# Softmax sums of an attention kernel: one accumulating chain of transfers instead of three groups of matmuls

## The chip, the cores and the metric

One core of a Trainium2 chip runs the whole program. The metric is device time in microseconds (us). A kernel's time is the median of its runs. One further execution was recorded by the hardware profiler: its trace gives every instruction's start, duration and waits.

## The reference

The input is x of shape 2 x 2048 x 512. The part that matters here is attention with 16 heads of width 32 and 2 groups of keys and values:

```python
q = q * cos + rotate_half(q) * sin          # also k; k and v are shared by 8 heads each
scores = jnp.einsum('bqhd,bkhd->bhqk', q, k_exp) * hd ** (-0.5)
attn = jax.nn.softmax(scores, axis=-1)
out = jnp.einsum('bhqk,bkhd->bqhd', attn, v_exp).reshape(b, s, d)
return out @ wo + bo
```

A layer norm stands ahead of it and a residual addition behind it. A second layer norm and a product with weights that are rounded to 8 bits follow, and another residual addition.

## The kernel before

**Units.** The attention is cut into 64 units: 8 token blocks of 512 queries, 4 quads of heads in each, 2 halves of 256 queries (`HB`) in each quad. A unit runs over all 2048 keys of its batch in 16 chunks of 128 keys, four chunks to a round (`ROUND = 4`, `ROUNDS = 4`). The text calls the rounds of a unit block 0 to block 3. The order of instructions within a round is written out by hand in the program; every engine takes its own instructions strictly in that order.

**A round.** For each chunk PE multiplies the keys with the queries into `T` (L963; in chunks 0 and 1 a matmul with the negated maxima goes ahead, L954), and ACT takes the exponential into a tile `p` of 128 keys x (4 heads x 256 queries) (L972). There are four `p` buffers and two `T` buffers. POOL adds the tiles of two chunks into a tile `pa` (L946, `add_pair`). The first pair's tile is then added to the second pair's by an accumulating transfer that POOL issues (L1015). So a unit leaves four tiles `far_sums[0..3]`, one per round, each the sum of four chunks. In block 2 another accumulating transfer adds `far_sums[0]` to `far_sums[1]` (L1017). The pool of these tiles has four buffers, so a tile of a round is overwritten in the same round of the next unit. At the end of a round PE multiplies the four `p` tiles with the values into `avs[:, 0, :]` (`columns`, L913; 32 records).

**Sums.** The softmax denominators need the sum over the 128 partitions as well. PE does this with a matrix of ones (`sum_up`, L927), 4 matmuls for each tile, into `avs[:, 1, :]` of the next unit: `far_sums[1]` and `far_sums[2]` at the end of that unit's block 0, `far_sums[3]` at the end of its block 1. The trace shows two records for each of these fp32 matmuls.

**Division.** ACT copies the products of a unit into the tile `both[:, 0, :]` at the unit's end (L1033). `finish_heads` copies the sums into `both[:, 1, :]` (L885, ACT), takes reciprocals in two pieces (L889, DVE) and multiplies (L890, POOL) into `attn`. The tile `both` has one buffer:

```python
            both = w2.tile([P, 2, HB], F32, tag="both", name=f"both_{u}", bufs=1)
            nc.scalar.copy(both[:, 0, :], avs[:, 0, :])
            far_before = far_sums
```

**Work ahead and side jobs.** The softmax's maxima for the next unit are found one unit ahead: PE makes scores `s` (L517) and DVE reduces them (L524), 8 pairs of instructions in each round, called at fixed places of the round (`next(scores, None)`). Three PSUM banks hold them, one of which is lent to a side job while that needs it. Side jobs are projections of coming blocks, rope, the output product with `wo`, the second layer norm. They wait in queues, and `fill` takes a step of one where the round has a place for it: `fill(ON_PE)` in the middle of a round, `fill(ON_DVE, 3 if finishing else 2)` at its end. A job of the list `finishing` (the division) goes first. At the start of every second unit ACT splits the next queries into a high part (L246) and POOL subtracts it for the low part (L247). SP's queue carries the other transfers.

Of the kernel before, what the change touches and what calls it, by code (L numbers as in the profile page):

```python
# [13 lines left out]
ALU = mybir.AluOpType  # L14
# [13 lines left out]
def preln_attn_fp8_ffn_kernel(  # L28
# [37 lines left out]
    nc = tc.nc  # L66
# [403 lines left out]
    units = [(k, half) for k in range(len(quads)) for half in range(HALVES)]  # L470
# [28 lines left out]
    def split_maxima():  # L499

        if split:
            mview, mx = split.pop()
            nc.gpsimd.tensor_tensor(
                mview[:, :, :, 1], mx, mview[:, :, :, 0].bitcast(F32), ALU.subtract
            )
# [257 lines left out]
    def fill(kind, pieces=1):  # L763

        for _ in range(pieces):
            ready = [job for job in queue if job.due <= step[0] and not job.waits()]
            if lent[0] is not None:
                ready = [job for job in ready if job is owner[0]]
            able = [
                (jobs, job)  # L770
                for jobs, some in ((finishing, finishing[:1]), (queue, ready), (beside, beside))
                for job in some
                if job.kind in (kind, OTHER) and job.due <= step[0]
            ]
            if able:
                do(*able[0])
# [41 lines left out]
    def stack_next(u):  # L818
        k, half = units[u]
        n, quad = quads[k]  # L820

        if half == 0:
            if k + 1 < len(quads) and k + 1 not in qst:
                while quads[k + 1] not in q_raw:
                    advance()
                stack_queries(k + 1)
        b = batch(k)
        if b + 1 < B and n == (b + 1) * NB - 1 and quad == 2 and half == 1:
            while (b + 2) * NB - 1 not in keys_done:
                advance()  # L830
            fetch_keys("kS", b + 1, 0)
            fetch_keys("dkS", b + 1, 0)
        if b > 0 and n == b * NB and quad == 0 and half == 0:
            fetch_keys("kS", b, 1)
            fetch_keys("dkS", b, 1)
# [69 lines left out]
    def columns(u, chunks, probs, av):  # L905

        k, half = units[u]
        for kc, p in zip(chunks, probs):
            if kc == NTS - 2 and u + 1 < len(units):
                tp = ps_t.tile([P, 4 * HB], F32, tag="E", name=f"mtp_{u + 1}")  # L910
                gather_maxima(u + 1, tp)
            for j in range(4):
                nc.tensor.matmul(  # L913
                    av[j * HD : (j + 1) * HD, :],
                    vX[batch(k)][:, kc, group(k), :],
                    p[:, j, :],
                    start=(kc == 0),
                    stop=(kc == NTS - 1),
                    tile_position=(0, j * HD),
                    skip_group_check=True,  # L920
                )

    def sum_up(dst, parts, start, stop):

        for i, part in enumerate(parts):
            for j in range(4):
                nc.tensor.matmul(  # L927
                    dst[j * HD : (j + 1) * HD, :],
                    ones,
                    part[:, j, :],  # L930
                    start=start and i == 0,
                    stop=stop and i == len(parts) - 1,
                    tile_position=(0, j * HD),
                    skip_group_check=True,
                )

    def add_pair(u, kc, a, b):
        far = kc % ROUND == 2
        pa = papool.tile(
            [P, 4, HB],  # L940
            F32,
            tag="pa" if far else "pair",
            name=f"pa_{u}_{kc}",
            bufs=4 if far else 2,
        )
        nc.gpsimd.tensor_tensor(pa, a, b, ALU.add)  # L946
        return pa

    def probabilities(u, T, kc):

        k, half = units[u]
        if kc < 2:
            for j in range(4):
                nc.tensor.matmul(  # L954
                    T[:, j, :],
                    sel[:, j, :],
                    maxima[u],
                    start=(j % 2 == 0),
                    stop=True,
                    skip_group_check=True,  # L960
                )
        for j in range(0, 4, 2):
            nc.tensor.matmul(  # L963
                T[:, j : j + 2, :],
                stacked["dkS"][:, group(k), kc * P : (kc + 1) * P],
                qst[k][:, j : j + 2, half * HB : (half + 1) * HB],
                start=False,
                stop=True,
                skip_group_check=True,
            )  # L970
        p = ppool.tile([P, 4, HB], F32, tag="p", name=f"p_{u}_{kc}")
        nc.scalar.activation(p, T, AF.Exp, scale=SCALE)  # L972
        return p

    with tc.manual_schedule():
        for _ in range(LEAD):
            next(scores)
        for u, (k, half) in enumerate(units):
            n, quad = quads[k]
            if half == 0 and quad == 0:  # L980
                attn_of[n] = wide.tile(
                    [P, QUADS, TB], F32, tag="attn", name=f"attn_{n}", bufs=2
                )
            stack_next(u)
            banks = [
                ps_t.tile([P, 4, HB], F32, tag="EO"[parity], name=f"T_{u}_{parity}")
                for parity in range(2)
            ]

            far_sums = []  # L990
            whole = u == len(units) - 1
            ending_soon = u >= len(units) - 2
            pieces = 2 if ending_soon else 1
            for r in range(ROUNDS):
                chunks = list(range(r * ROUND, (r + 1) * ROUND))
                step[0] += 1
                while r == 1 and landing:
                    landing.pop()()
                if r == 2:
                    ask(u)  # L1000
                last = r == ROUNDS - 1
                next(scores, None)
                probs = [probabilities(u, banks[kc % 2], kc) for kc in chunks[:2]]
                pair = add_pair(u, chunks[0], *probs)
                next(scores, None)
                if r > 0:
                    fill(ON_PE, pieces)
                probs.append(probabilities(u, banks[0], chunks[2]))
                next(scores, None)
                probs.append(probabilities(u, banks[1], chunks[3]))  # L1010
                if ending_soon:
                    fill(ON_DVE)
                if not (last and whole):
                    far_sums.append(add_pair(u, chunks[2], *probs[2:]))
                    nc.gpsimd.dma_start(out=far_sums[r], in_=pair, accum_op=ALU.add)  # L1015
                if r == 2:
                    nc.gpsimd.dma_start(out=far_sums[1], in_=far_sums[0], accum_op=ALU.add)  # L1017
                fill(ON_PE, pieces)
                next(scores, None)
                split_maxima()  # L1020
                fill(ON_DVE, 3 if finishing else 2)
                if r == 0:
                    avs = ps_av.tile([P, 2, HB], F32, tag="av", name=f"avs_{u}")
                columns(u, chunks, probs, avs[:, 0, :])


                if u > 0 and r == 0:
                    sum_up(avs[:, 1, :], far_before[1:3], False, False)
                elif u > 0 and r == 1:
                    sum_up(avs[:, 1, :], far_before[3:], False, True)  # L1030
                    finishing.append(Job(finish_heads(u - 1, both, avs[:, 1, :])))
            both = w2.tile([P, 2, HB], F32, tag="both", name=f"both_{u}", bufs=1)
            nc.scalar.copy(both[:, 0, :], avs[:, 0, :])  # L1033
            far_before = far_sums
        sums = ps_s.tile([P, TB], F32, tag=s_bank(), name="sums_last")[:, :HB]
        sum_up(sums, [pair, *probs[2:], *far_sums[1:]], True, True)
        finishing.append(Job(finish_heads(u, both, sums)))
        fetch_y_over_keys(2, "kS", 1)
        attending[0] = False
        for jobs in (finishing, queue, beside):  # L1040
            while jobs:
                jobs[0].step()
                if jobs[0].kind is None:
                    jobs.pop(0)
# [122 lines left out]
```

## Time and profile before

| | us |
|---|---|
| median of 3 runs | 2333.15 (2331.62 to 2337.78) |
| the profiled execution | 2336.02 |
| its span, first to last instruction | 2334.2 |

| engine | busy us | share of the span |
|---|---|---|
| PE | 2143.7 | 92% |
| POOL | 1765.1 | 76% |
| DVE | 1698.0 | 73% |
| ACT | 1237.0 | 53% |

The units lie between 127 and 2225 us of the span; most take 33 to 34 us, those without side jobs 28 to 29 us. In that stretch the granted TensorE clock is 0.99. A row of the page's groups has the line, the engine, the operation, the tiles (written <- read), the count, the busy time, the mean of one in ns, and the idle time ahead of them with what ended it. Matmul ends are modelled: a busy PE is not a PE at its peak, and the starts are what can be trusted. Spans on POOL are rough, and neighbouring ones overlap.

### The profile page before, as it was taken

What the parts mean: (1) busy time and instruction counts of PE and PEld (TensorE: products, weight loads), DVE (VectorE), ACT (ScalarE), POOL (GpSimd) and SP (SyncE); (2) the same over time, 40 slices, a digit from 0 to 9 for tenths busy, and PEclk for the clock granted to TensorE, in tenths of its full rate; (3) what the DMA queues carried; (4) which work ended last, traced back from release to release, by engine and by line L of the source; (5) the groups of instructions that cost most, each with busy time, mean ns of one, the idle gap of its engine ahead of it and who ended that gap; (6) DMA issues with size and microseconds to landing.
All of it is one profiled execution on the core that took longest, in us unless ns stands there. A gap on an engine that the chain in (4) does not pass through costs nothing. (4 is left out here: it accounts for less than half of the span.)

```text
span 2334.2 us, 39403 instructions
## 1 busy us (share of the span) xinstructions
PE 2143.7 (92%) x15506; PEld 1242.2 (53%) x15506; DVE 1698.0 (73%) x2679; ACT 1237.0 (53%) x1545; POOL 1765.1 (76%) x1199
## 2 busy tenths in 40 slices
PE   5499999999999999999999999999999899899955
PEld 3255555555555555555555555555555455555522
DVE  3467778776777776876767778676877977767578
ACT  2146556655556555655445456555555555545646
POOL 3268889888878987888868878887888777877810
PEclk9599999999999999999999999999999999999978
DMA  6546656666465765659586456664665645847512
GB/s 204 160 102 128 141 114 161 140 142 131 100 163 130 159 129 136 145 115 197 103 202 137 102 127 136 147 112 96 133 154 123 138 101 115 170 98 197 109 52 112
DMA packets 116411, 312.78 MB, mean 134 GB/s; under 512 B 16896, under 2 KB 17536, under 8 KB 112384
## 3 DMA queue, kind: packets, MB, share of 16 engines
q0 software_dynamic: 50160, 175.66, 40.0%
q1 hardware_dynamic: 63648, 133.21, 19.2%
q8 instruction: 122, 2.00, 0.3%
q10 hardware_dynamic: 2416, 1.38, 0.2%
q14 instruction: 65, 0.53, 0.1%
HBM read 91.56 MB, written 42.99 MB: 58 GB/s over the span
## 5 line engine op out<-in xcount | busy, mean ns | idle before, releaser
L524 DVE TENSOR_REDUCE part<-s 128x1 f32<-128x512 f32 x2048 | 1304.2, 684 | 541.8 <-PE s L517 528.8
L946 POOL TENSOR_TENSOR pa<-p,p 128x1024 f32<-128x1024 f32 x511 | 1234.9, 2466 | 293.1 <-ACT p L972 265.8
L972 ACT ACTIVATE p<-T 128x1024 f32<-128x1024 f32 x1024 | 1001.4, 1024 | 597.8 <-PE T L963 564.6
L517 PE MATMUL s<-kS,qst 128*128 128x512 f32 x2048 | 832.1, 465 | 87.6 <-DVE part L524 28.7
L963 PE MATMUL T<-qst,dkS 128*128 128x512 f32 x2048 | 669.5, 423 | 11.8 <-ACT p L972 11.8
L517 PEld LDWEIGHTS s<-kS,qst 128*128 128x128 f32 x2048 | 369.7, 190 | 478.0 <-DVE part L524 266.5
L913 PE MATMUL avs<-p,vX 128*32 128x256 f32 x8192 | 509.4, 383 | 0.8 <-ACT p L972 0.8
L963 PEld LDWEIGHTS T<-qst,dkS 128*128 128x128 f32 x2048 | 366.0, 189 | 159.8 <-ACT p L972 54.8
L913 PEld LDWEIGHTS avs<-p,vX 128*32 128x32 f32 x8192 | 233.1, 109 | 214.4 <-issue 79.6
L1015 POOL DMA_DIRECT2D pa<-pa x255 | 224.2, 879 | 80.3 <-POOL pa L946 75.6
L301 PE MATMUL po<-wo_sb,attn 128*128 128x512 f32 x256 | 130.7, 596 | 1.3 <-POOL attn L890 1.3
L889 DVE RECIPROCAL both<-both 128x128 f32<-128x128 f32 x128 | 112.4, 920 | 11.2 <-ACT both L885 11.2
L301 PE MATMUL pq<-xnT_q,wq_sb 128*128 128x512 f32 x224 | 114.3, 592 | 0.0
L927 PE MATMUL avs<-pa,ones 128*32 128x256 f32 x1512 | 105.5, 382 | 5.5 <-DMA pa<-pa 5.5
L885 ACT COPY both<-avs 128x256 f32<-128x256 f32 x63 | 23.5, 372 | 132.8 <-PE avs L927 132.8
L890 POOL TENSOR_TENSOR attn<-both 128x256 f32<-128x256 f32 x64 | 85.2, 1331 | 5.9 <-DVE both L889 5.9
L954 PEld LDWEIGHTS T<-mT,sel 128*128 128x128 f32 x512 | 78.7, 190 | 13.6 <-ACT mT L546 1.9
L954 PE MATMUL T<-mT,sel 128*128 128x256 f32 x512 | 82.2, 283 | 1.1 <-ACT mT L546 1.1
L1017 POOL DMA_DIRECT2D pa<-pa x64 | 74.2, 1159 | 3.9 <-DMA pa<-pa 3.6
L927 PEld LDWEIGHTS avs<-pa,ones 128*32 128x32 f32 x1512 | 49.2, 111 | 38.6 <-DMA pa<-pa 6.0
L546 ACT CAST mT<-mtp 128x256 fp32r<-128x256 f32 x64 | 23.9, 373 | 84.0 <-PE mtp L542 84.0
L532 ACT CAST mrow<-mx 128x8 fp32r<-128x8 f32 x64 | 13.1, 205 | 93.5 <-DVE mx L531 93.5
(126 smaller groups left out, 1160.8 us busy)
## 6 DMA issues: line engine op xcount, KB each, us to landing
pa<-pa POOLq DMA_DIRECT2D x319, 512.0 KB, 4.9
qst<-q_far SPq DMA_DIRECT2D x128, 256.0 KB, 4.3
x_kv<-in_L_attn_x_dram SPq DMA_DIRECT2D x8, 1024.0 KB, 8.8
q_far<-hi_q SPq DMA_DIRECT2D x32, 256.0 KB, 4.4
q_far<-lo_q SPq DMA_DIRECT2D x32, 256.0 KB, 3.7
x_res<-in_L_attn_x_dram SPq DMA_DIRECT2D x8, 1024.0 KB, 8.2
x_res<-in_L_attn_bo_dram POOLq DMA_DIRECT2D x8, 1024.0 KB, 11.6
out_dram<-v SPq DMA_DIRECT2D x16, 512.0 KB, 2.8
```

The lines of the kernel that those rows point to most:

```text
L301: nc.tensor.matmul(dst, lhs(c), rhs(c), start=(c == 0), stop=(c == chunks - 1))
L517: nc.tensor.matmul(s, qst[k][:, j, at : at + P], stacked["kS"][:, group(k), kb * TB : (kb + 1) * TB], start=True, stop=True,)
L524: nc.vector.tensor_reduce(part[:, i, j, kb : kb + 1], s, AX.X, ALU.max)
L889: nc.vector.reciprocal(piece, piece)
L890: nc.gpsimd.tensor_tensor(attn_of[n][:, quad, half * HB : (half + 1) * HB], both[:, 0, :], both[:, 1, :], ALU.mult)
L913: nc.tensor.matmul(av[j * HD : (j + 1) * HD, :], vX[batch(k)][:, kc, group(k), :], p[:, j, :], start=(kc == 0), stop=(kc == NTS - 1), tile ...
L927: nc.tensor.matmul(dst[j * HD : (j + 1) * HD, :], ones, part[:, j, :], start=start and i == 0, stop=stop and i == len(parts) - 1, tile_pos ...
L946: nc.gpsimd.tensor_tensor(pa, a, b, ALU.add)
L954: nc.tensor.matmul(T[:, j, :], sel[:, j, :], maxima[u], start=(j % 2 == 0), stop=True, skip_group_check=True,)
L963: nc.tensor.matmul(T[:, j : j + 2, :], stacked["dkS"][:, group(k), kc * P : (kc + 1) * P], qst[k][:, j : j + 2, half * HB : (half + 1) * H ...
L972: nc.scalar.activation(p, T, AF.Exp, scale=SCALE)
L1015: nc.gpsimd.dma_start(out=far_sums[r], in_=pair, accum_op=ALU.add)
```

## The change

For the units 0 to 60 the tiles are summed by transfers down to one: in block 0 of the next unit, after its first addition, POOL issues an accumulating transfer that adds `far_sums[1]` to `far_sums[2]`, and in block 1 one that adds `far_sums[2]` to `far_sums[3]`. PE then multiplies `far_sums[3]` alone with the ones, at the end of block 2, and the division's job starts there. The last units keep the old way. The line numbers behind the change are 4 to 9 higher in the changed kernel.

```diff
+    def in_one(u):
+
+        return 0 <= u < len(units) - 3
...
                 pair = add_pair(u, chunks[0], *probs)
+
+                if r < 2 and in_one(u - 1):
+                    at = r + 2
+                    nc.gpsimd.dma_start(
+                        out=far_before[at], in_=far_before[at - 1], accum_op=ALU.add
+                    )
                 next(scores, None)
...
-                if u > 0 and r == 0:
+                if u > 0 and r == 0 and not in_one(u - 1):
                     sum_up(avs[:, 1, :], far_before[1:3], False, False)
-                elif u > 0 and r == 1:
+                elif u > 0 and r == (2 if in_one(u - 1) else 1):
                     sum_up(avs[:, 1, :], far_before[3:], False, True)
                     finishing.append(Job(finish_heads(u - 1, both, avs[:, 1, :])))
```

## The prediction

> **What bounds the kernel.** I read the page's busy times first, then the waits, then the timeline around the place where one unit ends and the next begins, last the windows of single units.
>
> ```profile
> PE 2143.7 (92%) x15506; PEld 1242.2 (53%) x15506; DVE 1698.0 (73%) x2679; ACT 1237.0 (53%) x1545; POOL 1765.1 (76%) x1199
> ```
>
> PE looks full, but its ends are modelled. What the waits say is that the others wait for PE far longer than PE waits for them:
>
> ```profile
> ACT p L972 <- PE T L963: 564.6, 409, 11.5
> DVE part L524 <- PE s L517: 528.8, 560, 12.3
> PEld s L517 <- DVE part L524: 266.5, 668, 5.4
> POOL pa L946 <- ACT p L972: 265.8, 202, 12.6
> ```
>
> The columns are the total, the number of waits and the longest, in us. So a round runs at PE's pace, with short waits of PE for DVE's reductions. The timeline at a unit's end (PE, DVE, ACT, POOL in turn) shows what the change touches:
>
> ```profile
> 1248.05 0.65 PE L963 MATMUL T<-qst,dkS 128*128 128x512 f32 x2
> ...
> 1253.32 1.05 PE L927 MATMUL avs<-pa,ones 128*32 128x256 f32 x16
> 1254.30 0.73 PE L517 MATMUL s<-kS,qst 128*128 128x512 f32 x2
> ```
> ```profile
> 1242.63 1.29 DVE L524 TENSOR_REDUCE part<-s 128x1 f32<-128x512 f32 x2 [0.50 <-PE s L517]
> ```
> ```profile
> 1245.32 0.37 ACT L1033 COPY both<-avs 128x256 f32<-128x256 f32 x1 [0.71 <-PE avs L913]
> 1245.59 0.62 ACT L246 CAST hi_q<-q 128x512 fp32r<-128x512 f32 x1
> 1246.89 2.92 ACT L972 ACTIVATE p<-T 128x1024 f32<-128x1024 f32 x3 [0.68 <-PE T L963]
> ```
> ```profile
> 1242.70 2.38 POOL L946 TENSOR_TENSOR pa<-p,p 128x1024 f32<-128x1024 f32 x1 [0.27 <-ACT p L972]
> 1245.38 0.89 POOL L1015 DMA_DIRECT2D pa<-pa  x1 [0.30 <-POOL pa L946]
> ```
>
> PE's third-chunk scores (1248.05) start 0.14 us after the unit's first exponential ends (1246.89 + 1.02): that exponential is on the path at every unit's start. The sums' 16 records hold PE from 1253.32 to 1254.30. POOL's last addition of the old unit ends at 1245.08, 0.24 us before the copy. A unit with no side jobs looks different:
>
> ```profile
> 383.76:412.12 28.36, 27.80 (x227) 16.75 (x227) 21.67 (x35) 17.45 (x21) 24.07 (x16) 1.00 0.92 239
> ```
>
> In 28.36 us POOL is busy 24.07, and the DMA engines have a share of 0.92 (the column before the last). Its last addition ends at 415.44, over 3 us after the copy at 412.12. Today nobody waits for that.
>
> **The change, part by part.** All against the profiled execution, 2336.02 us (span 2334.2), 2.9 above the median. The order of instructions of the changed program confirms the matmuls left out, two more DMAs a unit on POOL, and where the rest moves.
>
> *Sums, removed.* 8 of 12 matmuls, 16 records, leave block 0 of 61 units: 1254.30 - 1253.32 = 0.98 us each, so -59.8 us if PE sets the end there. The last 4 go from block 1 to block 2: nothing.
>
> *Reciprocals.* They leave the end of block 2 for the end of block 3, where DVE is idle for 1.06 us shortly after. The second s pair of a block cost 0.85 us after reciprocals (1238.24) and 0.72 without (1221.38): -0.13 x 61 = -8. Bounds 0 and -0.5 a unit, the latter from the uncluttered unit where reductions begin at 406.06, 1.26 us behind their matmul.
>
> *The new wait.* "both" has one buffer. Unit u-1's division used to end in block 2 of unit u; now the reciprocals come after block 3's reductions and the multiplication after block 3's second addition and its DMA issue, just ahead of ACT's copy of unit u into the same "both". ACT is in order: behind the copy stand the hi/lo split of q (every second unit) and all exponentials of the next unit, and PE's T of chunk 2 waits for the first of them. The multiplication takes 0.73 us when it is not queued (its shortest is 0.725).
> Case on time (37 of 61 ends, last addition within 0.85 us of the copy, mostly at -0.24): DVE decides. Last reduction ends at -0.72 relative to the old copy, reciprocals +1.7, semaphore 0.1, multiplication 0.73, semaphore 0.08: copy at 1.86, first exponential 0.3 later, at 2.15 instead of 1.57: +0.58, or +1.11 with the split of q in front. In block 0 PE has about 0.85 us of waits for DVE after that place (s at 1248.76 and s at 1250.61 take 0.93 and 0.96 us for 0.47 of work), which hide the first whole and leave 0.3 of the second: 16 x 0.3 = +5.
> Case late: at 24 ends the last addition ends 1.05 to 3.74 us after the copy, mean 2.38. With the multiplication moved behind the additions (0.70 us earlier in the queue before) 1.69 remain. Then 0.30 wait and 0.60 issue of L1015, 0.73, 0.08, 0.27 of copy, less 1.57: 2.10, with the split at half of them 2.36 of delay; 0.6 is hidden (0.4 in units without side jobs, 0.85 in others): 1.76 x 24 = +42. Bounds: 0.75 lateness where POOL holds no backlog at all (block 3's second pair of exponentials ends 4.05 before the copy, two additions take 4.8), which gives +20; nothing hidden, +57.
> The Trainium skill (Perfetto Trace Analysis, Optimization Strategy) reads a gap that repeats as a possible sign of too few buffers for the next tile. Before, the copy waited 42.4 us on PE and 0.7 on POOL, so no row shows that gap yet. By the page a second buffer would take the +47 of these two cases away, and the change would be worth its -60.
>
> *Two DMA issues on POOL*, in blocks 0 and 1, 0.60 to 0.88 us each (L1015 to the next instruction, 0.60; its mean 0.879), with the additions, rope, the hi/lo split and the rest behind them. In 49 units POOL idles later in the unit for the exponentials and absorbs them. In 12 it has been busy without a break since block 1: 12 x 0.6 to 1.2, take +8. The waits in front of them (the transfer before has landed) are covered: landing takes 4.7 to 6.8 us, a block 6.4 to 8.7. PE meets the chain about 11 us after its last issue.
>
> *DMA time.* q0 is busy 40% of 2334 us for 327 accumulating transfers: 2.8 us of all 16 engines each, 5.6 more per unit. Read unit by unit, the share is 0.41 to 0.7 mostly; three units (0.92, 0.94, 0.94 of 28 to 32 us) would need 3 to 4 us more than they have, +10. Eight have 0.80 to 0.89 and would come to about 1: between 0 and one transfer each, 0 to +22, take +6. Sum +16, bounds 0 and +32.
> The Trainium skill (DMA: Bandwidth & Descriptors, Anatomy of one DMA) fits 2.0 us plus bytes over 436 GB/s to a transfer issued by GpSimd. By that my estimate of the occupied part is 1.2 us for 512 KB, no unit would be over-full and the sum 16 lower. The row says 2.8.
>
> *DVE's side jobs.* Where two of them follow block 0's reductions (DVE has no gap from 1251.44 to 1257.51), the next block's scores wait for DVE, and some 0.35 us of the 0.98 is not gained: about 20 units, +7, bounds 0 and +12.
>
> Sum: -59.8 - 8 + 5 + 42 + 8 + 16 + 7 = +10: 2346 in an execution like the profiled one, 2343 as a median. About 0.3%, 7 us, is what a measurement of this kernel can tell from no change.
>
> **Rivals.**
> *Faster: POOL catches up.* Every unit now starts with POOL free, since the copy waited for it, so a backlog is not carried on as it is today; late ends fall to the bound of +20, the issues cost nothing, the DMA term is halved. -59.8 - 8 + 5 + 20 + 8 + 7 = -28: 2305. For it: in 37 of 61 ends POOL is on time, with 3 to 8 us of idle time in such units. Against: the late ones are units where POOL is at 85% of the time, and it now idles at each start for about 2.4 us, until two new exponentials are done. It decides from a mean lateness below 1.2 us at those 24 ends.
> *No change.* PE's 0.98 us and ACT's delay cancel everywhere: 2333. For it: the sum is a difference of terms of 50 to 70 us. Against: only by accident.
> *Much slower: the DMA engines.* Where SP loads x, queries and keys, landings already reach 14 us, POOL's L1017 waits up to 3.6 us, and it waits in order; with the upper DMA bound (+32) and nothing hidden at late ends (+57) the sum is +41: 2374. Against: median landings of 4.5 to 5 us.
> *The change not doing what it says* is excluded by the instruction order.
>
> **How the numbers follow.** Forecast case 0.52, own range 2334 to 2384, of which 0.44 lie above 2340; POOL catches up 0.30 (2298 to 2326); cancelling 0.10; DMA 0.08. Faster 0.30, same 0.18, slower 0.52. The range 2304 to 2384 leaves out the lower edge of the second case and the outer part of the last, together under 0.2.
>
> **What would show it.** Right: a line of the waits "ACT both <- POOL attn" over some 60 copies, about 1.5 us each; L927 with 976 records fewer; units without side jobs longer than 28.4 to 29 us, those of 33 to 34 shorter by 0.5 to 1; POOL's issues of the chain about 122 x 0.9. Wrong: the copies wait for POOL by less than 0.7 us on average (then faster); units without side jobs not longer; PE's wait for DVE's reductions grown by more than 20 us (then the 0.98 was not PE's to gain); waits for "DMA pa<-pa" grown by over 30 us (then the third rival).

## The result, and the profile after

The changed kernel takes 2426.40 us (median of 4 runs, 2425.35 to 2430.82) against 2332.39 before (2326.82 to 2337.78). The ratio is 1.0402 with a 95% interval of 1.0388 to 1.0416: 94 us slower. The forecast was 2343 with a range up to 2384. The direction was right, and the size was outside the range.

The profiled execution of the changed kernel took 2430.82 us, its span is 2429.1. The page begins with the engines (busy us, share of the span, instructions):

```profile
PE 2126.9 (88%) x14530; PEld 1235.8 (51%) x14530; DVE 1720.3 (71%) x2679; ACT 1227.7 (51%) x1545; POOL 1875.1 (77%) x1321
```

PE has 976 records fewer, as forecast, and POOL is busy 110 us longer. The waits (total, count, longest) that are new or have grown:

```profile
ACT both L1042 <- POOL attn L890: 204.9, 61, 6.6
PEld T L967 <- ACT p L976: 155.2, 182, 4.8
PE T L967 <- ACT p L976: 94.7, 111, 4.4
POOL pa L1011 <- DMA pa<-pa: 39.7, 20, 6.7
PEld avs L931 <- DMA pa<-pa: 33.1, 11, 5.5
POOL pa L950 <- DMA pa<-pa: 27.8, 18, 4.3
```

Before, the T row for ACT's exponentials was

```profile
PEld T L963 <- ACT p L972: 54.8, 158, 1.3
```

So ACT's copy into `both` now waits for POOL's multiplication at each of 61 units, and the copy's lateness reaches PE through the exponentials. The last three rows are waits for landings of accumulating transfers, the chain's among them; POOL's wait of L950 was 16.2 and PE's of L931 6.0 before. Two groups of the page show the prices on POOL and ACT (columns: count, busy us, mean ns, idle us ahead and what ended it):

```profile
L1011 POOL DMA_DIRECT2D pa<-pa x122 | 108.2, 887 | 39.7 <-DMA pa<-pa 39.7
L1042 ACT COPY both<-avs 128x256 f32<-128x256 f32 x64 | 23.8, 372 | 207.5 <-POOL attn L890 204.9
```

Block lengths follow from the starts of PE's first T of every round, means over 61 units. Before, blocks 0 to 3 took 8.55, 7.87, 7.71 and 8.77 us; after, 9.01, 7.70, 8.94 and 8.69. Block 0 lost 16 matmul records and still grew; block 2, where PE meets the chain, grew by 1.23 us a unit. Some 0.31 of this come with the last matmuls and the division, which stand there now: in a kernel with this move and no chain (late_two, below) block 2 takes 8.03 us.

The granted clock fell too: between the starts of units 1 and 62 it was at a half for 24 us in 4 stretches before, and for 126 us in 28 stretches after. The last section shows one such stretch.

### The profile page after: what moved, and what is told of

Its sections match the earlier page's. It is cut to its first block, busy times and chain, and to the rows that moved or that the text cites. A ratio compares the mean times of both kernels' runs of the same rounds, so it can differ in the third digit from the quotient of the medians.

```text
span 2429.1 us, 37636 instructions
## 1 busy us (share of the span) xinstructions
PE 2126.9 (88%) x14530; PEld 1235.8 (51%) x14530; DVE 1720.3 (71%) x2679; ACT 1227.7 (51%) x1545; POOL 1875.1 (77%) x1321
## 4 chain that ended last, share of the span: by engine, by line
PE 40%; POOL 21%; DMA 12%; DVE 11%; ACT 7%; issue 5%; SPq 1%; DVEq 0%; ACTq 0%; POOLq 0%
POOL pa L950 14%; PE s L517 12%; PE T L967 10%; DMA pa<-pa 9%; PE avs L913 9%; ACT p L976 6%; DVE part L524 4%; PE po L301 3%; PE pq L301 3%; DVE sw_q L319 2%; POOL attn L890 2%; POOL pa L1024 2%; PE avs L931 1%; POOL pa L1011 1%; DMA sw_q<-q 1%
## 5 line engine op out<-in xcount | busy, mean ns | idle before, releaser
L950 POOL TENSOR_TENSOR pa<-p,p 128x1024 f32<-128x1024 f32 x511 | 1274.1, 2536 | 213.7 <-ACT p L976 181.0
L976 ACT ACTIVATE p<-T 128x1024 f32<-128x1024 f32 x1024 | 998.3, 1024 | 574.8 <-PE T L967 531.2
L517 PE MATMUL s<-kS,qst 128*128 128x512 f32 x2048 | 821.7, 467 | 87.3 <-DVE part L524 41.8
L967 PE MATMUL T<-qst,dkS 128*128 128x512 f32 x2048 | 695.4, 437 | 95.0 <-ACT p L976 94.7
L517 PEld LDWEIGHTS s<-kS,qst 128*128 128x128 f32 x2048 | 381.2, 196 | 441.7 <-DVE part L524 227.0
L913 PE MATMUL avs<-p,vX 128*32 128x256 f32 x8192 | 519.8, 388 | 8.8 <-ACT p L976 8.5
L913 PEld LDWEIGHTS avs<-p,vX 128*32 128x32 f32 x8192 | 233.8, 111 | 235.7 <-issue 82.2
L1024 POOL DMA_DIRECT2D pa<-pa x255 | 223.2, 875 | 82.8 <-POOL pa L950 79.1
L1011 POOL DMA_DIRECT2D pa<-pa x122 | 108.2, 887 | 39.7 <-DMA pa<-pa 39.7
L1042 ACT COPY both<-avs 128x256 f32<-128x256 f32 x64 | 23.8, 372 | 207.5 <-POOL attn L890 204.9
L889 DVE RECIPROCAL both<-both 128x128 f32<-128x128 f32 x128 | 112.4, 919 | 11.9 <-ACT both L885 11.9
L1026 POOL DMA_DIRECT2D pa<-pa x64 | 73.8, 1154 | 2.1 <-PE s L517 1.7
L890 POOL TENSOR_TENSOR attn<-both 128x256 f32<-128x256 f32 x64 | 66.3, 1036 | 6.5 <-DVE both L889 6.5
L885 ACT COPY both<-avs 128x256 f32<-128x256 f32 x63 | 23.5, 373 | 91.9 <-PE avs L931 91.9
L931 PE MATMUL avs<-pa,ones 128*32 128x256 f32 x536 | 43.2, 399 | 27.8 <-DMA pa<-pa 27.8
L319 DVE SCALAR_TENSOR_TENSOR sw_q<-sw_q,sign,cs 128x512 f32<-128x512 f32 x30 | 66.6, 2221 | 0.4 <-issue 0.4
## 6 DMA issues: line engine op xcount, KB each, us to landing
x_res<-in_L_attn_bo_dram POOLq DMA_DIRECT2D x8, 1024.0 KB, 11.9
```

Source lines behind the costliest of these rows:

```text
L319: nc.vector.scalar_tensor_tensor(t[:rows], t[:rows], sign[:rows], csb[:rows, 1, :], ALU.mult, ALU.mult)
L517: nc.tensor.matmul(s, qst[k][:, j, at : at + P], stacked["kS"][:, group(k), kb * TB : (kb + 1) * TB], start=True, stop=True,)
L890: nc.gpsimd.tensor_tensor(attn_of[n][:, quad, half * HB : (half + 1) * HB], both[:, 0, :], both[:, 1, :], ALU.mult)
L913: nc.tensor.matmul(av[j * HD : (j + 1) * HD, :], vX[batch(k)][:, kc, group(k), :], p[:, j, :], start=(kc == 0), stop=(kc == NTS - 1), tile ...
L967: nc.tensor.matmul(T[:, j : j + 2, :], stacked["dkS"][:, group(k), kc * P : (kc + 1) * P], qst[k][:, j : j + 2, half * HB : (half + 1) * H ...
L1011: nc.gpsimd.dma_start(out=far_before[at], in_=far_before[at - 1], accum_op=ALU.add)
```

## The experiments

All differences below are against the median of the kernel before in the same comparison. The first four undo or do one part alone.

**The division moved, nothing else.** Kernel before; the last four matmuls and the division go one block later, and `both` keeps its one buffer:

```diff
-                elif u > 0 and r == 1:
+                elif u > 0 and r == (2 if u < len(units) - 2 else 1):
```

> The kernel before, with the sums of far_sums[3] and the division that follows moved from block 1 to block 2 for the same units as in the change; all 12 matmuls stay, no transfer is added. Theory of the late copy (ACT's copy into the one buffer of both waits for the division, and the exponentials behind it are late): +1.2 to +1.5 us a unit, 2400 to 2425 us, with a wait of ACT both on POOL attn of some 3 us at 61 copies. Rival of the transfers (the two more accumulating transfers and their issue on POOL cost the time): within 10 us of the kernel before, 2322 to 2342.

Measured: 2374.35, ratio 1.0171 (1.0154 to 1.0188), +41. The waits of this kernel hold the same row as those of the changed one:

```profile
ACT both L1033 <- POOL attn L890: 186.4, 59, 5.7
PEld T L963 <- ACT p L972: 151.0, 192, 4.4
```

The late copy is there with no transfer added: 3.2 us at 59 copies, as that theory said. The time lies between the two ranges of the expectation.

**Eight matmuls left out.** Kernel before; `sum_up` of `far_sums[1:3]` is left out for units 0 to 60:

```diff
-                if u > 0 and r == 0:
+                if u > 0 and r == 0 and u >= len(units) - 2:
```

> The kernel before without the 8 matmuls of block 0 in 61 units (the sums of two tiles are left out, nothing takes their place). If the 0.98 us of PE in block 0 is PE's to gain: 2332 - 55, about 2270 to 2285. Rival (DVE's reductions or the exponentials end the block anyway): above 2315.

Measured: 2288.11, ratio 0.9815 (0.9792 to 0.9838), -45. Block 0 became 0.96 us shorter, as the 0.98 of the trace says, but block 1 grew by 0.25: the next scores wait for DVE.

```profile
PEld s L517 <- DVE part L524: 274.7, 674, 6.7
```

This row was 266.5 before. 0.25 x 61 = 15 us of the gain are given back, where the prediction had 7; the row holds 8 of them.

**Two buffers of `both`.** Changed kernel:

```diff
-            both = w2.tile([P, 2, HB], F32, tag="both", name=f"both_{u}", bufs=1)
+            both = w2.tile([P, 2, HB], F32, tag="both", name=f"both_{u}", bufs=2)
```

> The changed kernel with two buffers for both. Theory of the late copy: the copy no longer waits for POOL, and most of the loss goes: 2290 to 2345. Rival of the transfers: above 2395, because POOL's issues and the landings are the same.

Measured: 2366.54, ratio 1.0152 (1.0122 to 1.0181), still +33 against before, and 61 below the changed kernel when both are taken against their own runs of before (94.0 - 33.4). This lies between the two ranges of the expectation. The copy no longer waits for POOL, but the landings remain:

```profile
ACT both L1042 <- PE avs L913: 40.0, 60, 1.2
PEld avs L931 <- DMA pa<-pa: 38.4, 10, 6.3
POOL pa L950 <- DMA pa<-pa: 37.4, 20, 5.1
POOL pa L1011 <- DMA pa<-pa: 36.2, 16, 6.3
```

So more than the new wait was wrong in the sum. By the starts of T, 37 of 61 units became shorter than before, by 1 us in the mean, and a dozen grew by 3 to 10 us, in all but one of them (unit 6) most of it in block 2. In most of these SP moves tiles of 1 MB, tables or keys. Unit 56 is one. The DMA row of that unit (2004 to 2036 us of the span, 40 slices of 0.8 us, busy tenths of the 16 DMA engines):

```profile
DMA  9999008999994769999999999999999999999918
```

From 2016 to 2034 us there is no free slice. The timeline of SP's and POOL's queues at that place (start, duration, instruction, idle time before it in brackets):

```profile
2016.93 1.61 SPq L141 DMA_DIRECT2D x_res<-in_L_attn_x_dram  x2
```
```profile
2021.45 0.87 POOL L1011 DMA_DIRECT2D pa<-pa  x1 [1.35 <-DMA pa<-pa]
2022.06 2.68 POOL L950 TENSOR_TENSOR pa<-p,p 128x1024 f32<-128x1024 f32 x1
2025.04 0.86 POOL L1024 DMA_DIRECT2D pa<-pa  x1 [0.30 <-POOL pa L950]
...
2027.93 2.34 POOL L950 TENSOR_TENSOR pa<-p,p 128x1024 f32<-128x1024 f32 x1 [0.59 <-DMA pa<-pa]
```

Two loads of 1 MB fall on the chain. POOL holds the second issue until the first transfer has landed, and later the additions whose buffer a transfer still reads or writes.

**The chain one block earlier,** to give it more time to land; sums in block 1, division as before. First transfer at the end of the unit's own block 3, second in the next unit's block 0:

```diff
+                if r == 0 and in_one(u - 1):
+                    nc.gpsimd.dma_start(out=far_before[3], in_=far_before[2], accum_op=ALU.add)
...
+                if last and in_one(u):
+                    nc.gpsimd.dma_start(out=far_sums[2], in_=far_sums[1], accum_op=ALU.add)
```

> The changed kernel with the chain one block earlier: the first of the two transfers at the end of the unit itself (block 3), the second in block 0 of the next unit, PE's 4 matmuls and the division back in block 1 and 2. Same number of transfers and issues as in the change. Theory of the late copy: no wait of the copy, PE's saving stays: 2285 to 2330, below the kernel before. Rival of the transfers: 2395 or more.

A miss: 2487.36, +154. Now POOL stands in order for the first transfer at almost every unit, and ACT's exponentials wait behind the additions that this delays:

```profile
POOL pa L1010 <- DMA pa<-pa: 164.0, 53, 11.4
ACT p L976 <- POOL pa L950: 258.4, 107, 12.8
```

The next four ask what the transfers cost, and where. In the first of them the two issues are left out of the changed kernel (`pass` in their place), with one buffer of `both`.

> The changed kernel without the chain's 122 transfers; the sums of far_sums[1] and far_sums[2] are left out of the denominators, PE's 4 matmuls of far_sums[3] stay in block 2 and 'both' keeps one buffer. If the three costs add up (sums removed -44, late copy +41, the rest the transfers), the time is 2325 to 2340, about 90 below the changed kernel. If the transfers are cheap, as the prediction's +16 and +8 had it, the time stays above 2390. The waits of L931 and L950 for 'DMA pa<-pa' (33 + 28 and 28 us) should go, the copy's wait for POOL's attn (205 us) should stay or shrink a little.

Measured: 2338.27, +5, so 89 of the 94 us go with the transfers, and the copy's wait stays (189.2 us over 60 copies).

For the second, with two buffers, only the direction of the second transfer changes:

```diff
-                        out=far_before[at], in_=far_before[at - 1], accum_op=ALU.add
+                        out=far_before[to], in_=far_before[of], accum_op=ALU.add
```

(`to, of` is 2, 1 in block 0 and 2, 3 in block 1.)

> The changed kernel with two buffers of 'both', and the second transfer reversed: it adds far_sums[3] into far_sums[2] instead of the other way. So as many transfers of the same size, issued at the same places, but PE's 4 matmuls read far_sums[3], which no transfer writes any more (far_sums[1] and [2] are left out of the denominators). Theory A, PE waits at its meeting with the chain for a late landing: the 72 us of waits of L931 go and the time falls from 2367 to 2285 to 2310. Theory B, the transfers cost by occupying POOL and the DMA engines, wherever they land: 2350 or more. Between them, the part above 2290 is what POOL's waits and the DMA engines cost.

Measured: 2356.61, +23. PE's landing waits are gone, and only 10 us with them. Others take over, as a group of waits of this kernel shows:

```profile
ACT p L976 <- POOL pa L950: 101.2, 54, 8.0
POOL pa L950 <- DMA pa<-pa: 44.9, 22, 5.5
```

By the starts of T, block 2 is 0.58 us a unit shorter than in the kernel with two buffers and block 3 is 0.30 longer. In block 3 ACT's exponentials wait 31 us for POOL's additions, against 5: POOL is held up by landings as before (the additions 44.9 us against 37.4), and ACT now meets the delay where PE had met the chain. The time fits the second theory of the expectation, but the experiment does not show which part is POOL's and which the DMA engines'.

**The chain only where it was not longer.** Two buffers; `in_one` is false for the 21 units that had grown:

```diff
-        return 0 <= u < len(units) - 3
+        return 0 <= u < len(units) - 3 and u + 1 not in LOUD
```

> The changed kernel with two buffers of 'both', and the old way (12 sum matmuls, no chain) in the 21 units that were longer with the chain than before; 41 or so units keep the chain. If the cost sits in those units alone, where the DMA engines were already busy for 80% and more, the time is 2285 to 2310, below the kernel before (2333). If the cost is spread over all units, or moves to other units when these are spared, 2325 to 2350.

Measured: 2299.45, ratio 0.9855 (0.9833 to 0.9877). This is 34 us below the kernel before, and the fastest kernel of this study that leaves nothing out.

**One transfer in place of two,** in the kernel before: `far_sums[1]` into `far_sums[2]` in block 0, PE sums two tiles in block 1.

> The kernel before with one extra transfer a unit: far_sums[1] into far_sums[2] in block 0; PE sums far_sums[2] and far_sums[3] (8 matmuls) at the end of block 1, where the last 4 were; the division stays where it was, so no late copy. PE saves 4 matmuls a unit, about half of the 44 us. If a chain of two dependent transfers is what lands late, one alone with some 11 us to land costs little: 2310 to 2330. If a transfer costs by its mere bytes, half of the chain's price comes: 2340 to 2365.

Measured: 2334.34, ratio 1.0002 (0.9992 to 1.0012). Half the matmuls gained and one transfer a unit cancel out. The time lies 4 us above the first case's range. With half of the 45 us gained, the one transfer costs about 24 (estimate), less than a third of the 89 that the two cost.

**Fewer bytes.** The two-buffer kernel with the two transfers cut to 128, or to 512, of 1024 elements a row:

```diff
-                        out=far_before[at], in_=far_before[at - 1], accum_op=ALU.add
+                        out=far_before[at][:, 0, :128], in_=far_before[at - 1][:, 0, :128], accum_op=ALU.add
```

> The changed kernel with two buffers of 'both' (2367), the chain's two transfers cut to 128 of 1024 elements a row: the same issues at the same places, the same order and the same waits, an eighth of the bytes; 7/8 of two tiles is left out of the denominators. Theory A, the transfers cost by the bytes that the DMA engines have to move: what is left is two issues on POOL a unit and the time is 2288 to 2305. Theory B, they cost by POOL's issues and by waiting in order: 2345 or more.

> As thin_chain, with 512 of 1024 elements a row. If the DMA engines' price is a saturation (nothing until a unit has no room left), half the bytes cost clearly less than half of the distance between thin_chain and 2367: 2300 to 2320. If it is in proportion to the bytes, about 2330.

Measured: 2330.44 (-3) and 2341.91 (+8), full +33. An eighth to a half of the bytes adds 11 us, a half to all of them 25: the bytes' price grows faster than the bytes (the half lies above both ranges of its expectation, all the same). But theory A expected 2288 to 2305 with an eighth of the bytes, so 25 to 42 us did not go with the bytes.

**Eleven units, chosen by the trace of before,** spared (`quiet_rule`) or alone (`loud_only`); the same edit as above with `LOUD = {8, 12, 20, 28, 29, 32, 40, 42, 48, 56, 60}`, and with `in LOUD` for the reverse.

> The changed kernel with two buffers of 'both', and the old way in the eleven units whose DMA share in the trace of the kernel before was 0.80 or more (8, 12, 20, 28, 29, 32, 40, 42, 48, 56, 60); a choice from the trace of before alone. In the kernel with two buffers and the chain everywhere, these units were 58 us longer than before in sum. If the price lies in them, the time is 2300 to 2318; if it moves on to other units, 2330 or more.

> The reverse of quiet_rule: the chain in those eleven units alone, the old way in the other 50. If the price lies in the eleven, the time is 2375 to 2395, above that of the chain everywhere with two buffers (2367) although only 22 of 122 transfers are left. If it is spread over all transfers, 2335 to 2345.

Measured: 2320.17 (-14, ratio 0.9953, 0.9936 to 0.9969) and 2373.52 (+40, 1.0178, 1.0163 to 1.0193). The eleven units together cost 40 us with 22 transfers, the other 50 gain 14 with 100. (The 58 us in the expectation was a wrong sum: these units were 50 us longer.) `loud_only` fell 1.5 us below its range and `quiet_rule` 2 above; the place of the price is as stated.

**Where the price without bytes is.** With two buffers: no transfers at all, and the two issues with few bytes and no dependence of the second on the first (it adds `far_sums[3]` to itself), once with full and once with thin transfers.

```diff
-                        out=far_before[at], in_=far_before[at - 1], accum_op=ALU.add
+                        out=far_before[at], in_=far_before[at - 1 + r], accum_op=ALU.add
```

> The changed kernel with two buffers of 'both' and without the chain's transfers (far_sums[1] and [2] are left out of the denominators). It is the end of the row full, half and an eighth of the bytes (2367, 2342, 2330). If transfers with few bytes still cost through POOL (two issues, the second waiting for the first), the time is 2285 to 2300, near the kernel before without its 8 matmuls (2288), and the 30 to 45 us up to 2330 are POOL's. If the rest of 2330 comes from the division's new place, it is 2315 to 2330.

> The changed kernel with two buffers of 'both', the second transfer adding far_sums[3] to itself instead of far_sums[2] to it (so the denominators hold twice far_sums[3] alone): as many full transfers and issues, the same landing for PE to meet, but POOL no longer waits in order for the first transfer to land before it issues the second. If POOL's in-order wait (36 us at L1011, and the exponentials behind it) is a main part of the price, 2325 to 2345; if bytes on the DMA engines are all that counts, it stays at 2360 to 2370.

> self_add with 128 of 1024 elements a row: two issues a unit on POOL, hardly any bytes, no wait for the first landing. What it lies above no_chain_two is the price of the bare issues: by the prediction's row (0.6 to 0.88 us each, 12 units without cover) 8, so 2293 to 2308 if no_chain_two is near 2290; if POOL has no room in many more units, 2315 or more.

Measured: 2275.29 (-56), 2366.10 (+35) and 2318.35 (-13). The issues with an eighth of the bytes cost 43 us (-13.0 + 56.1), where the prediction had 8 for the issues. Not all of it is POOL's time: PE still waits for a landing in four units (5.5 us). With full transfers, taking away POOL's in-order wait for the first one brings nothing (+35 against +33); with thin ones it brings 10 (thin_chain less thin_self). The page's groups show one part of the 43, first without the transfers, then with the thin ones:

```profile
L319 DVE SCALAR_TENSOR_TENSOR sw_q<-sw_q,sign,cs 128x512 f32<-128x512 f32 x30 | 47.8, 1592 | 0.4 <-DMA sw_q<-q 0.2 <-issue 0.2
```
```profile
L319 DVE SCALAR_TENSOR_TENSOR sw_q<-sw_q,sign,cs 128x512 f32<-128x512 f32 x30 | 69.3, 2311 | 0.4 <-DMA sw_q<-q 0.2 <-issue 0.2
```

DVE's rope step L319 is not changed at all, and became 0.72 us longer (21.5 us in all). The timelines of one such place, unit 15, say why: first without, then with the issue.

```profile
609.40 2.38 POOL L950 TENSOR_TENSOR pa<-p,p 128x1024 f32<-128x1024 f32 x1 [0.23 <-ACT p L976]
...
610.53 1.79 DVE L319 SCALAR_TENSOR_TENSOR sw_q<-sw_q,sign,cs 128x512 f32<-128x512 f32 x1
```
```profile
621.28 0.86 POOL L1011 DMA_DIRECT2D pa<-pa  x1
621.89 2.66 POOL L950 TENSOR_TENSOR pa<-p,p 128x1024 f32<-128x1024 f32 x1
...
622.66 2.45 DVE L319 SCALAR_TENSOR_TENSOR sw_q<-sw_q,sign,cs 128x512 f32<-128x512 f32 x1
```

In both, L319 ends about 0.55 us after POOL's addition ends (612.32 against 611.78, 625.11 against 624.55). The issue pushes that addition back, and L319's end moves with it, in this unit with POOL idle later on. Block 1 of unit 15 is 0.65 us longer. The 21 blocks that come right behind a lengthened L319 grew by 29 us together, of the 43; the rest lies in block 2 of other units and was not followed up.

**The issues behind the round's second addition,** in the kernel with thin, independent transfers, so that neither addition is pushed back.

> thin_self (2318) with the two issues moved behind the round's second addition and its transfer, out of the gap between the two additions. In the trace of thin_self, DVE's L319 ends about 0.55 us after the POOL addition that runs beside it, and that addition starts 0.6 later because of the issue: L319 took 2311 ns instead of 1592 (no_chain_two, 30 of them, 21.6 us), about half of the 43 us that the bare issues cost. If L319's wait for POOL is that half, it falls back to about 1600 to 1800 ns and the time to 2290 to 2305. If the issues cost by POOL's time alone, wherever they stand, 2313 to 2323.

Measured: 2450.68, +120, a miss in the time, with the part that it was made for as expected. L319 falls back, but a new wait outweighs it (groups, then waits):

```profile
L319 DVE SCALAR_TENSOR_TENSOR sw_q<-sw_q,sign,cs 128x512 f32<-128x512 f32 x30 | 51.5, 1717 | 0.4 <-DMA sw_q<-q 0.2 <-issue 0.2
```
```profile
POOL pa L950 <- DMA pa<-pa: 124.0, 42, 9.0
PE avs L931 <- DMA pa<-pa: 72.1, 32, 7.3
```

In nine units whose block 1 had grown by 0.63 to 0.69 us with the issues (7, 15, 23, 31, 34, 36, 42, 44, 50), block 1 is back within 0.02 us of the kernel without transfers. So in block 1 of these units the price was that of L319 behind the pushed addition, not of POOL's time. The transfers, issued some 3 us later, now land when the next round's addition wants the buffer, even with an eighth of the bytes: the chain's place fits between two waits, and one step either way costs over 100 us (chain_earlier against the two-buffer kernel, and this one against its own).

**The division's new place with all matmuls,** two buffers: the kernel before with both edits of the first and third experiment, and `quiet_units` with the new place in its old-way units too.

> The kernel before with the last 4 sum matmuls and the division one block later and two buffers of 'both'; all 12 matmuls kept, no chain. no_chain_two (2275) lies 13 below the kernel before without 8 matmuls (2288): if that is the division's new place, this kernel is at 2315 to 2325. If it comes only together with the missing matmuls, 2328 to 2338.

> quiet_units (2299) with the division one block later in its 21 old-way units too. If the new place is worth 13 over 61 units, about 4 are left for these: 2290 to 2300, and it is the fastest of the correct versions. If the place is worth nothing there, 2299 again or a little more.

Measured: 2316.76 (-19, ratio 0.9919, 0.9901 to 0.9938) and 2309.37 (-26). The place alone, with a second buffer, is a gain. The last one is a miss: 10 us behind `quiet_units`, for a reason not followed up.

## Why the prediction was right in direction and wrong in size

The kernels of the last column lead step by step from the kernel before to the changed one, so their differences add up to the 94 us by construction. Another order could price a step otherwise: the division's new place with a second buffer brings 11 us without the eight matmuls and 19 with them (late_two).

| term | predicted | measured | from |
|---|---|---|---|
| 8 matmuls out of block 0, less what DVE takes back | -59.8 + 7 | -45 | no_block0_sums |
| reciprocals, sums and division one block later | -8 | -11 | no_chain_two less no_block0_sums |
| late copy | +5 + 42 | +61 | changed kernel less two_both |
| two issues on POOL (measured with an eighth of the bytes) | +8 | +43 | thin_self less no_chain_two |
| DMA time and landings | +16 | +46 | two_both less thin_self |
| sum | +10 | +94 | |

All terms but the second were off to the same side, so that the errors add up and none hides another.

**The late copy: mechanism right, 14 short.** Three pairs of kernels that differ in the buffer alone give 60 or 61 (also late_division less late_two, no_chain less no_chain_two). By the starts of T and of the exponentials in late_division and late_two, the delay at the 24 late ends is 2.32 us, inside the 2.10 to 2.36 that was worked out. In this pair 2.05 us of it reach the unit's length at these ends, not 1.76, and at the 37 punctual ends 0.36 us each, not 0.14 (16 x 0.3 over 37). (The prediction's terms for a punctual end add up to 1.89, not 1.86; nothing hangs on it.) The excess goes with the clock: eleven units that have a stretch at half clock in one of the two kernels make 33 of 63 us (by the starts of T), and without them it is 1.30 us at late ends and 0.31 at punctual ones. The prediction had drawn from the Trainium skill (Perfetto Trace Analysis, Optimization Strategy), where a repeated gap can mean too few buffers, that a second buffer takes this gap away. That holds: it takes 61. That the change would then be worth its -60 does not: it is still +33.

**The matmuls.** PE's 0.98 us in block 0 is confirmed at 0.96. DVE takes back 15 and not 7.

**The issues: the worst-sized term, 35 short.** The step that failed is "In 49 units POOL idles later in the unit ... and absorbs them". Idle time later in a unit pays POOL back. It does not pay those who wait for the pushed addition: DVE's L319 at once, and ACT's exponentials for the `p` buffer (that wait grew from 30.9 to 55.1 us between no_chain_two and thin_self). With the thin issues, 33 of 61 units are over 0.5 us longer, not 12. Shown by an experiment is the part of L319 in nine units (issue_behind, some 6 us); for the rest of the 43 the mechanism is argued from the traces.

**DMA time: 30 short.** The occupied time was right: the q0 shares of two_both and no_chain_two (53.7% of 2377.0, 41.2% of 2272.0) differ by 2.8 us for each of 122 transfers, as the row of before said, and not by the 1.2 worked out from the Trainium skill (DMA: Bandwidth & Descriptors, Anatomy of one DMA). What failed is the step from there to time. The share was taken over a unit, so that only an over-full unit paid. But SP's loads come in bursts: in unit 56 there was no free slice from 2016 to 2034 us. "PE meets the chain about 11 us after its last issue" was taken as cover, and PE met late landings in ten units of two_both and eleven of the changed kernel, 3 to 4 us each in the mean and 6.3 at the longest. The eleven units with a share of 0.80 or more were rightly picked out: they cost 40 us (loud_only).

**The clock: a term that the sum does not have.** The prediction reckoned with the clock of before. PE of the changed kernel stops more often (29 times for over 2 us between the starts of units 1 and 62, 4 times before), and stretches at half clock follow its stops. An estimate of what they cost at most is half of their length: 12 us before, 63 after. So up to 51 of the 94 us can be theirs, within the terms above: up to 31 of the 46 for DMA time and landings (two_both 48, thin_self 17), up to 19 of the 60 for the late copy (late_division 26, late_two 7), and up to 7 of the 43 for the issues (no_chain_two 10). No experiment separates a stop of PE from the slower matmuls behind it. But 20 units that have such a stretch in two_both or thin_self make 59 of the 60 us between these two by the starts of T.

**The marks.** The copies' wait for POOL was forecast as about 1.5 us at some 60 copies; it is 3.4 (204.9 / 61), of which 1.57 us reach the first exponential by its start against PE's T. All twelve units below 29.2 us but one became longer, as stated. Of the 19 units of 33 to 34 us only 4 became shorter by 0.5 us or more; their mean is 0.7 longer.

**The rivals.** The prediction's own mark for the third rival was met: POOL's waits for landings rose from 20 to 68 us, PE's from 5.5 to about 30. Its price, +41, was too low too: it raised the DMA term to 32 and the late ends to 57 and left the issues at 8. The first rival, POOL catching up, fell: POOL's last addition does end before every copy (2.0 us in the mean), but only because the copy now waits for POOL.

## What to carry to other kernels

An instruction put ahead of another on an in-order engine is not free where that engine idles later: look at who waits for the instruction that is pushed back, on the other engines too. A mean DMA share over a stage hides bursts: lay the new transfers over the slices in which the large loads run, and name for each new transfer who needs its two tiles next and how soon. Where PE stops, read the granted clock behind the stop as well: the stop can cost more than its own length. Where a user of a single-buffered tile moves late, give it a second buffer in the same change; here that alone turned +41 into -19.

## What the runs showed of the hardware

DVE's L319 reads two operands in SBUF, and of its 30 instances in a trace nearly all that begin beside a running POOL operation end about 0.55 us after that operation's end, up to 3.5 us long (a few wait for POOL's next operation too: the longest took 5.2 in thin_self and 6.4 in two_both); the shortest, with no POOL operation beside them, take 0.65. The page of the Trainium skill on this is SBUF — State Buffer, Who interferes with whom: a DVE instruction with two SBUF inputs contends with a GpSimd instruction that reads SBUF, and the port pair that they share is an exclusive lock. The traces agree, and show what follows: an operation of POOL that stands beside this instruction of DVE makes it up to five times as long (3.5 against 0.65 us), and more where it meets a second one.

A transfer with an eighth of the bytes (64 KB) lands in a median of 3.0 us, but in up to 11.9 us beside SP's loads; a full one (512 KB) in 5.6 and up to 13.9. So the longest landings go with the traffic beside a transfer more than with its own size.

Stretches at half clock follow stops of PE. Each of the 17 of two_both and the 28 of the changed kernel begins behind 3.4 us in which PE was busy for less than half of the time, and lasts 3.4, 6.8 or 10.2 us. Unit 12 of two_both has one from 540.54 to 547.36 us. First PE's timeline, with a stop of 4.47 us, then the same stretch with the granted clock (the third number from the right):

```profile
537.51 0.50 PE L517 MATMUL s<-kS,qst 128*128 128x512 f32 x1
542.48 0.79 PE L517 MATMUL s<-kS,qst 128*128 128x512 f32 x1 [4.47 <-ACT q L450]
543.20 3.64 PE L913 MATMUL avs<-p,vX 128*32 128x256 f32 x32
546.62 0.98 PE L931 MATMUL avs<-pa,ones 128*32 128x256 f32 x8
```
```profile
540.54:547.36 6.82, 4.88 (x41) 2.07 (x41) 0.88 (x2) 2.61 (x5) 6.82 (x6) 0.50 0.81 153
```

The 32 records of L913 take 3.64 us here and 1.86 before, the 8 of the sums 0.98 us, in which PE did 16 before. The unit is 5.8 us longer than before: the stop and the slower matmuls behind it.
